# Two graph layers over a 4096 x 4096 adjacency: sums kept in more PSUM banks, more places for tiles, and a fixed order of the second sweep

## Chip, cores and metric

One core of one Trainium2 chip runs the whole program. The metric is the device time of one execution in microseconds (us), lower is better. A profiled execution, taken apart from the timed runs, gives the trace.

## What is computed

N = 4096 nodes, 64 features, a weighted adjacency `adj` (fp32, 67.1 MB) with about 0.8% of its entries not zero.

```python
# layer 0
h = relu(layernorm(x))
for k in range(2):
    agg = adj @ h
    h = tanh(concat([agg, h], 1) @ W[k])
x = x + h
# layer 1
h = relu(layernorm(x))
support = h @ weight
mask = adj != 0
rank = cumsum(mask, axis=1); deg = rank[:, -1:]
k = minimum(deg, 100)
pos = rank - (deg - k)
w = mask * where(pos > 0, 0.5 ** (k - pos), 0)
x = x + w @ support + bias
```

In layer 1 the last nonzero entry of a row weighs 1, the one before it 1/2, and so on.

## The kernel before

**Tiling.** The rows of the result are cut in four chunks of 1024 (index I or g, NCH = 4), the columns in 32 blocks of 128 (b), which also form four chunks of eight (J). A tile is one block against one chunk of rows: 128 x 1024 fp32, 512 KB.

**Sweep 1** (lines 464 to 611) loads all of `adj` once, in pairs of tiles. For each it does hop 1 of layer 0 (and hop 2 where the features of hop 1 are ready already, line 593), and it counts nonzeros, which leaves one byte per entry in `code[g][J]` (8 KB per partition for each of the 16 pairs). Places in these byte arrays that are not yet written serve as tile buffers, as the five pairs of `ring` do.

**Sweep 2** (lines 912 to 1036) does two things side by side.

- *Hops.* 72 tiles are loaded again and multiplied with the features of hop 1: `hop` (line 959) calls `agg_pair` (line 278), two fp32 matmuls of 512 columns. `plan` (line 917) sets their order: row 3 is complete after hop 12, row 2 after hop 24, row 1 after hop 48, row 0 after hop 72. When a row is complete, `finish_x2` (line 660) runs a chain of short steps over TensorE (py, line 678), VectorE, ScalarE and GpSimd that ends with layer 1's features of that chunk, `feats[I]` (lines 724 and 725).
- *Units of layer 1.* 128 units (J, g, n): source chunk J, target rows g, block n of eight. `convert` (line 771) turns 128 x 1024 bytes into fp32r weights, in one ScalarE instruction (Exp, line 791) or in two on VectorE (lines 783 and 786, by way of one scratch tile, `bits`). `layer1` (line 839) then does two matmuls of 128 x 512 (line 851). J runs from 3 down to 0, since row 3's features come first. In some pairs (`kept`, line 761) the sum over J stays in its PSUM banks; after the others `evict` (line 870) copies it to SBUF or adds it there, two VectorE or ScalarE instructions. After J = 0, `finish_out` (line 888) multiplies by the layer's weight (pto, line 899), adds, and stores.

**What sets the order.** The program is scheduled at build time. `clock` holds a planned time for each engine, `use` advances it, and the loop at lines 996 to 1034 picks the next piece of TensorE's work from these clocks: a hop if its tile is planned to have landed, a unit if its weights are planned to be ready, changing from one kind to the other as rules at lines 1004 to 1013 say. 56 units are held back until the hops are over (`n_late`, line 924). `decode` (line 795) places conversions and the last byte subtractions (`settle`, line 452) on ScalarE and VectorE, with limits: how far ahead of TensorE (`lead`, `dlead`), and how near to a waiting chain (`gap`). On the chip each engine runs its own list in that order and waits by semaphores.

**Places.** A converted unit needs a 128 x 1024 fp32r place (`spaces`). They come from ring pairs no longer needed for loads (`consumed`, line 939), from the bytes of pairs (J, g) whose units are done (`pair_space`, line 747, two places each), from `after0`, `after1`, `hx1` and `hx2` when these are read for the last time, and from each unit's own place after its matmuls. `KEEP` = 4 of the five ring pairs go on being loaded. Two pairs' bytes hold `parts`, the sums in SBUF.

**PSUM.** Eight banks: `pacc` two tiles of two banks, `plow` two of one, `pone` the single banks "one" and "two".

**Queues.** All loads of `adj` are issued by SyncE in order: rows 3 to 1 at line 930, row 0, whose DRAM side is rearranged in four short pieces per partition, at line 934; the residual x at line 655; stores at line 909.

Of the kernel before, what the change touches and what calls it, by code (L numbers as in the profile page):

```python
# [19 lines left out]
P = 128  # L20
# [8 lines left out]
LOW = 138  # L29
# [15 lines left out]
def gnn_kernel(  # L45
# [614 lines left out]
    def finish_x2(I, acc):  # L660
# [11 lines left out]
        state["gap"] = 1.35, 2.2  # L672
        yield t

        pt = one(name="py")
# [84 lines left out]
    order = {3: (0, 1, 2, 3), 2: (3, 0, 1, 2), 1: (2, 3, 0, 1), 0: (0, 1, 2, 3)}  # L760
    kept = {(3, 3), (2, 2), (1, 0), (1, 1)}
# [7 lines left out]
    state = {"wide": True, "fetch": True, "done": 0, "lead": 5.0, "dve": False, "dlead": 2.0, "gap": (0.0, 0.0)}  # L769

    def convert(engine=None):
        i = len(made)
        J, g, n = units[i]
        spaces.sort(key=lambda v: v[1])
        w, t = spaces.pop(0)
        v = (J, g, n % 2)
        if v in settled:
            settle(settled.index(v))
            done[J, g] = use("DVE", 1.25)
        t = max(t, done.get((J, g), 0.0) + 0.1)  # L780
        q = code[g][J][:, n, :]
        if engine == "DVE" or not engine and state["dve"] and max(clock["ACT"], t) + 0.96 > max(clock["DVE"], t) + 1.4:
            nc.vector.tensor_scalar(  # L783
                state["bits"], q, float(ZERO), ONE, op0=ALU.subtract, op1=ALU.mult
            )
            nc.vector.tensor_scalar(  # L786
                w, state["bits"].bitcast(F32), 2.0 ** (127 - LOW), None, op0=ALU.mult
            )
            t = use("DVE", 1.4, t)
        else:  # L790
            nc.scalar.activation(w, q, AF.Exp, scale=LN2, bias=BIAS)  # L791
            t = use("ACT", 0.96, t)
        made.append([w, t + 0.1])

    def decode():
        while True:
# [8 lines left out]
            if n < len(units):  # L805
                wanted = {(J, g, k % 2) for J, g, k in units[n : n + 12]}
                soon = [v for v in settled if v in wanted]
            else:
                soon = []
            t = min((v[1] for v in spaces), default=1e9)  # L810
            if n == len(units):
                t = 1e9
            act, dve = (max(clock[e], t) for e in ("ACT", "DVE"))
            late = clock["DVE"] <= clock["PE"] + state["dlead"]
# [4 lines left out]
            elif (  # L819
                state["dve"] and late and dve + 1.4 <= d_end and dve <= clock["PE"] + 3.0  # L820
                and dve + 1.4 < act + 0.96 + (0.0 if len(spaces) < 3 else 1.0)
            ):
                convert("DVE")
            elif act <= min(now, a_end - 0.96):
                convert("ACT")
# [13 lines left out]
    def layer1():  # L839
# [3 lines left out]
        while len(made) <= i:  # L843
            convert()
        J, g, k = units[i]
        if k == 0 and g not in sums:
            sums[g] = pacc.tile([P, NC, C], F32, tag="acc", name="accl")
        first, last = k == 0 and (J + 1, g) not in kept, k == CB - 1 and (J, g) not in kept
        w = made[i][0]
        for c in range(NC):  # L850
            nc.tensor.matmul(  # L851
                sums[g][:, c, :], feats[J][:, k, :], w[:, c * C : (c + 1) * C],
                start=first, stop=last,
            )
# [5 lines left out]
        if 0 < J < NCH - 1 or J and g % 2:  # L860
            pair_space(f"code{g}{J}", t)
        elif J:
            parts[g // 2] = place([P, 2, NC, C], F32, f"code{g}{J}", "parts")
# [6 lines left out]
    def evict(J, g, acc):  # L870
# [3 lines left out]
        for c, p in enumerate(part(g)):  # L874
            if not new:
                nc.vector.tensor_tensor(p, acc[:, c, :], p, op=ALU.add)
                t = use("DVE", 0.7, t)
            elif clock["ACT"] <= clock["DVE"]:
                nc.scalar.copy(p, acc[:, c, :])
                t = use("ACT", 0.65, t)  # L880
            else:
                nc.vector.tensor_copy(p, acc[:, c, :])
# [3 lines left out]
    outs = []  # L886

# [24 lines left out]
    def sweep2(acc):  # L912
        rings = sorted(range(RING // 2), key=lambda k: places[k][2])
        KEEP = 4
# [9 lines left out]
        n_late = 56  # L924
        clock["DMA"] = -10.5

# [12 lines left out]
        def consumed(k, r, a, t):  # L939
            n = len(tiles)  # L940
            if k is None:
                state["bits"] = place([P, CW], U32, "hx0", "bits")
                state["dve"] = True
            elif n < total and (k in rings[-KEEP:] or n < 2 * RING - 2 * (RING // 2 - KEEP)):
                load(k, r, a, t)
            elif k in open_:
                pair_space(f"ring{k}", open_.pop(k), t)
# [3 lines left out]
        for n, k in enumerate(rings):  # L951
            for r in range(2):
                load(k, r, ring[k][:, r, :], 3.5 * (n - RING // 2 + 1))
# [5 lines left out]
        def hop(n):  # L959
            I, b = blocks[n]  # L960
            if I not in accs:
                accs[I] = two(name="acc1") if I == 1 else plow.tile([P, C], F32, tag="low", name="acc1")
# [23 lines left out]
        def runnable(cap, slack):  # L986
            n = 0
            for i in range(state["done"], min(cap, len(made))):
                t = max(ready.get(units[i][0], 1e9), made[i][1])
                if t > clock["PE"] + slack + 0.465 * n:  # L990
                    break
                n += 1
            return n

        n = 0
        while n < total or state["done"] < len(units) or chain or outs:
            run_chain()
            if n < total:
                state["lead"] = min(10.0, 0.86 * (total - n) + 0.2)
                state["dlead"] = min(2.0, state["lead"])  # L1000
            decode()
            if n == total:
                state.update(lead=10.0, dlead=2.0)
            cap = len(units) - (n_late if n < total else 0)
            units_ = runnable(cap, 0.1)
            hops = 0
            while n + hops < min(total, len(tiles)) and tiles[n + hops][3] <= clock["PE"] + 0.1 + 0.86 * hops:
                hops += 1
            if state["wide"]:
                go = 1 if units_ else 2 if hops else 0  # L1010
            else:
# [59 lines left out]
```

## Time and profile before

| | |
|---|---|
| median of 3 runs | 345.52 us (345.49, 345.52, 347.02) |
| the profiled execution's own time | 344.91 us |
| its span, first to last instruction | 343.0 us |
| TensorE matmul busy | 327.8 us (96%) |
| VectorE busy | 280.9 us (82%) |
| ScalarE busy | 197.0 us (57%) |
| HBM read, written | 107.15 MB, 1.05 MB: 315 GB/s over the span |
| last hop ends, last output matmul ends | 301.8 us, 339.5 us |

A page of the profile lists busy time by engine, the span in slices, the DMA queues, the chain of work that ended last, and the costliest groups. In a timeline, a row gives start, duration, engine, line, operation, output and inputs by the program's names, and how many instructions were merged in it; a bracket gives the idle time of the engine before the row and what ended it. One fp32 matmul of a hop shows as two records. Some matmul records are missing from the trace, so counts of them can be a few per cent low.

### The profile page before, as it was taken

What the parts mean: (1) busy time and instruction counts of PE and PEld (TensorE: products, weight loads), DVE (VectorE), ACT (ScalarE), POOL (GpSimd) and SP (SyncE); (2) the same over time, 40 slices, a digit from 0 to 9 for tenths busy, and PEclk for the clock granted to TensorE, in tenths of its full rate; (3) what the DMA queues carried; (4) which work ended last, traced back from release to release, by engine and by line L of the source; (5) the groups of instructions that cost most, each with busy time, mean ns of one, the idle gap of its engine ahead of it and who ended that gap; (6) DMA issues with size and microseconds to landing.
All of it is one profiled execution on the core that took longest, in us unless ns stands there. A gap on an engine that the chain in (4) does not pass through costs nothing.

```text
span 343.0 us, 3882 instructions
## 1 busy us (share of the span) xinstructions
PE 327.8 (96%) x1360; PEld 156.0 (45%) x1360; DVE 280.9 (82%) x440; ACT 197.0 (57%) x206; POOL 24.9 (7%) x23
## 2 busy tenths in 40 slices
PE   2899999999999999999999999999999999998995
PEld 0344334333444444344444343343454656367785
DVE  5799998999869999899998495688266799989953
ACT  2296872654466550474124534137378989979980
POOL 2450000000000000000000000422003000003000
PEclk9999999999999999999999999999999999999998
DMA  7999999999999998966998999999998958600012
GB/s 274 424 419 418 421 421 419 423 418 420 423 421 420 386 389 338 358 234 237 371 327 298 303 369 411 383 410 409 409 373 268 343 134 245 202 0 0 2 50 72
DMA packets 25474, 108.44 MB, mean 316 GB/s; under 512 B 2416, under 2 KB 3824, under 8 KB 17392
## 3 DMA queue, kind: packets, MB, share of 16 engines
q1 hardware_dynamic: 25456, 108.21, 82.7%
q8 instruction: 10, 0.16, 0.2%
q14 instruction: 8, 0.07, 0.0%
HBM read 107.15 MB, written 1.05 MB: 315 GB/s over the span
## 4 chain that ended last, share of the span: by engine, by line
PE 63%; DMA 21%; DVE 8%; ACT 3%; issue 2%; SPq 1%; ACTq 0%; DVEq 0%
PE acc L593 24%; PE acc L280 15%; PE accl L851 12%; DMA codes<-in_adjA_dram 11%; DMA ring<-in_adjA_dram 8%; PE acc_low L280 6%; DMA pre<-in_x_dram 2%; PE pto L899 2%; DVE weights L786 2%; ACT weights L791 2%; PE pt L348 2%; DVE bits L783 2%; PE po L211 1%; DVE mbuf L261 1%; DVE codes L253 1%
## 5 line engine op out<-in xcount | busy, mean ns | idle before, releaser
L791 ACT ACTIVATE weights<-codes 128x1024 fp32r<-128x1024 uint8 x90 | 86.7, 1046 | 12.2 <-PE accl L851 9.6
L593 PE MATMUL acc<-ring,hx 128*128 128x512 f32 x176 | 76.5, 594 | 0.6 <-DMA ring<-in_adjA_dram 0.6
L280 PE MATMUL acc<-ring,hx 128*64 128x512 f32 x288 | 66.8, 599 | 0.8 <-DMA ring<-in_adjA_dram 0.7
L851 PE MATMUL accl<-weights,feat 128*128 128x512 f32 x254 | 63.4, 400 | 1.3 <-DVE feat L725 0.9
L851 PEld LDWEIGHTS accl<-weights,feat 128*128 128x128 f32 x254 | 45.9, 188 | 21.3 <-ACT weights L791 6.6
L593 PEld LDWEIGHTS acc<-ring,hx 128*128 128x128 f32 x176 | 33.2, 190 | 43.8 <-issue 41.5
L456 DVE TENSOR_TENSOR codes<-codes,after 128x2048 uint16<-128x2048 uint16 x32 | 38.3, 1219 | 0.1
L280 PEld LDWEIGHTS acc<-ring,hx 128*64 128x64 f32 x288 | 19.3, 136 | 39.8 <-issue 29.8
L261 DVE TENSOR_SCALAR mbuf<-ring 128x2048 uint8<-128x2048 f32 x30 | 36.6, 1220 | 0.0
L246 ACT ACTIVATE codes<-codes 128x2048 uint8<-128x2048 int8 x18 | 34.4, 1910 | 0.6
L254 DVE TENSOR_SCALAR cnt<-codes 128x1024 uint16<-128x1024 uint16 (+1 forms) x80 | 30.0, 375 | 2.7
L253 DVE TENSOR_TENSOR codes<-mbuf,cnt 128x1024 uint16<-128x1024 uint16 (+1 forms) x51 | 30.6, 599 | 1.8
L786 DVE TENSOR_SCALAR weights<-bits 128x1024 fp32r<-128x1024 f32 x37 | 26.6, 718 | 6.6 <-PE accl L851 3.0
L245 ACT ACTIVATE codes<-ring 128x2048 int8<-128x2048 f32 x8 | 15.3, 1912 | 27.0 <-DMA ring<-in_adjA_dram 27.0
L783 DVE TENSOR_SCALAR bits<-codes 128x1024 uint32<-128x1024 uint8 x37 | 25.6, 691 | 0.8
L245 ACT ACTIVATE codes<-codes 128x2048 int8<-128x2048 f32 x10 | 19.1, 1913 | 11.7 <-DMA codes<-in_adjA_dram 11.6
L699 POOL TENSOR_TENSOR pre<-pre,wb 128x512 f32<-128x512 f32 x4 | 5.5, 1378 | 271.5 <-DVE xc L193 271.5
L280 PE MATMUL acc_low<-codes,hx 128*64 128x512 f32 x104 | 24.9, 594 | 0.1
L280 PE MATMUL acc_low<-ring,hx 128*64 128x512 f32 x88 | 22.3, 598 | 0.0
L545 PE MATMUL acc_low<-ring,hx 128*64 128x512 f32 x40 | 12.3, 745 | 8.3 <-DVE hx L201 6.8
L261 DVE TENSOR_SCALAR mbuf<-codes 128x2048 uint8<-128x2048 f32 x16 | 19.5, 1220 | 0.0
L198 POOL TENSOR_TENSOR s<-s,half 128x8 f32<-128x8 f32 (+1 forms) x10 | 16.9, 1691 | 15.7 <-DVE s L197 15.7
(99 smaller groups left out, 270.0 us busy)
## 6 DMA issues: line engine op xcount, KB each, us to landing
ring<-in_adjA_dram SPq DMA_DIRECT2D x74, 512.0 KB, 8.1
ring<-in_adjA_dram SPq DMA_DIRECT2D x37, 1024.0 KB, 8.0
codes<-in_adjA_dram SPq DMA_DIRECT2D x26, 1024.0 KB, 17.3
pre<-in_x_dram SPq DMA_DIRECT2D x4, 256.0 KB, 6.9
xres<-in_x_dram SPq DMA_DIRECT2D x4, 256.0 KB, 7.9
out_dram<-o SPq DMA_DIRECT2D x3, 256.0 KB, 2.6
out_dram<-o SPq DMA_DIRECT2D x2, 128.0 KB, 2.2
wb<-in_weights_dram SPq DMA_DIRECT2D x1, 192.0 KB, 14.3
```

Source lines behind the costliest of these rows:

```text
L245: nc.scalar.activation(sign, tile_of(I, a), AF.Sign)
L246: nc.scalar.activation(m, sign, AF.Square, scale=float((FLAG - 1 + 0.25) ** 0.5))
L253: nc.vector.tensor_tensor(q, m, cnt, op=ALU.add)
L254: nc.vector.tensor_scalar(cnt, q, 0x7F7F, None, op0=ALU.bitwise_and)
L261: nc.vector.tensor_scalar(m, tile_of(I, a), 0.0, float(FLAG - 1), op0=ALU.not_equal, op1=ALU.mult)
L280: nc.tensor.matmul(acc[c * D : (c + 1) * D, :], src, a[:, c * C : (c + 1) * C], start=first, stop=last,)
L456: nc.vector.tensor_tensor(q, q, a[:, None, :].to_broadcast([P, 4, CW // 2]), op=ALU.subtract)
L593: nc.tensor.matmul(acc[0][:, c, :], at(g), a[:, r, c * C : (c + 1) * C], start=g == CB * I - 1, stop=g == 0,)
L783: nc.vector.tensor_scalar(state["bits"], q, float(ZERO), ONE, op0=ALU.subtract, op1=ALU.mult)
L786: nc.vector.tensor_scalar(w, state["bits"].bitcast(F32), 2.0 ** (127 - LOW), None, op0=ALU.mult)
L791: nc.scalar.activation(w, q, AF.Exp, scale=LN2, bias=BIAS)
L851: nc.tensor.matmul(sums[g][:, c, :], feats[J][:, k, :], w[:, c * C : (c + 1) * C], start=first, stop=last,)
```

## The change

- **PSUM.** Nine of the twelve sums (J, g) with J > 0 are kept in PSUM over J, instead of four; the order of g within J changes. For the pairs (3, 2), (1, 1) and (0, 2) the sum lies in two tiles of `plow` instead of one of `pacc`. Row 0's hop accumulator moves from `plow` to the bank "one", and row 1's py from "one" to "two".
- **Places for tiles.** `more_tiles` turns the bytes of the finished pairs (3, 1), (2, 3), (2, 0) and (1, 0) into two load buffers each; if no load is left, they become places for weights. `KEEP` falls from 4 to 3, so that two ring pairs instead of one become places for weights early.
- **Conversions.** `convert` takes a list of engines. Two conversions on VectorE can be issued as two first halves and then two second halves if there are two scratch tiles in `bits`. A second one would come with the pair `bits_pair`, which is `None` in this version; `hx0` gives one scratch tile.
- **Order.** `steps2` lists (hops done, units done) eight times: hops up to the first number, then units up to the second. The rules on planned landings, `runnable` and `n_late` go.
- `lead` 10 to 6, `dlead` 2 to 3, `gap` ahead of the addition to py 1.35 to 0.5, and VectorE is chosen for a conversion with other margins.

```diff
-        state["gap"] = 1.35, 2.2
+        state["gap"] = 0.5, 2.2
...
-        pt = one(name="py")
+        pt = (two if I == 1 else one)(name="py")
...
-    order = {3: (0, 1, 2, 3), 2: (3, 0, 1, 2), 1: (2, 3, 0, 1), 0: (0, 1, 2, 3)}
-    kept = {(3, 3), (2, 2), (1, 0), (1, 1)}
+    order = {3: (0, 1, 2, 3), 2: (1, 2, 3, 0), 1: (2, 3, 0, 1), 0: (1, 0, 2, 3)}
+    spilled = {(3, 0), (2, 1), (1, 2)}
+    kept = {(J, g) for J in range(1, NCH) for g in range(NCH)} - spilled
+    in_low = {(3, 2), (1, 1), (0, 2)}
...
+        dve = [v for v in made_ if v[0] == "DVE"]
+        n = len(bits)
+        for k, (_, w, t, q) in enumerate(dve):
             nc.vector.tensor_scalar(
-                state["bits"], q, float(ZERO), ONE, op0=ALU.subtract, op1=ALU.mult
+                bits[k - n], q, float(ZERO), ONE, op0=ALU.subtract, op1=ALU.mult
             )
+            use("DVE", 0.65, t)
+        for k, (_, w, t, q) in enumerate(dve):
             nc.vector.tensor_scalar(
-                w, state["bits"].bitcast(F32), 2.0 ** (127 - LOW), None, op0=ALU.mult
+                w, bits[k - n].bitcast(F32), 2.0 ** (127 - LOW), None, op0=ALU.mult
             )
...
             elif (
-                state["dve"] and late and dve + 1.4 <= d_end and dve <= clock["PE"] + 3.0
-                and dve + 1.4 < act + 0.96 + (0.0 if len(spaces) < 3 else 1.0)
+                len(bits) > 1 and late and dve2 + 2.6 <= d_end and dve2 <= clock["PE"] + 3.0 and n + 2 <= len(units)
+                and len(spaces) > 1 and dve2 + 2.6 < act + 1.92 + (0.5 if len(spaces) < 4 else 2.0)
             ):
-                convert("DVE")
+                convert(["DVE", "DVE"])
+            elif (
+                bits and late and dve + 1.5 <= d_end and dve <= clock["PE"] + 3.0
+                and dve + 1.5 < act + 0.96 + (0.5 if len(spaces) < 3 else 2.0)
+            ):
+                convert(["DVE"])
...
-            sums[g] = pacc.tile([P, NC, C], F32, tag="acc", name="accl")
+            if (J, g) in in_low:
+                sums[g] = [plow.tile([P, C], F32, tag="low", name="accl") for _ in range(NC)]
+            else:
+                v = pacc.tile([P, NC, C], F32, tag="acc", name="accl")
+                sums[g] = [v[:, c, :] for c in range(NC)]
...
-        if 0 < J < NCH - 1 or J and g % 2:
+        if (J, g) in ((3, 0), (2, 2)):
+            parts[g // 2] = place([P, 2, NC, C], F32, f"code{g}{J}", "parts")
+        elif (J, g) == bits_pair:
+            v = place([P, 2, CW], U32, f"code{g}{J}", "bits")
+            bits[:] = [v[:, r, :] for r in range(2)]
+            space(place([P, CW], F32R, "hx0", "weights"), clock["DVE"] + 0.1)
+        elif (J, g) in tile_pairs:
+            more_tiles[0](f"code{g}{J}", t)
+        elif J:
             pair_space(f"code{g}{J}", t)
-        elif J:
-            parts[g // 2] = place([P, 2, NC, C], F32, f"code{g}{J}", "parts")
...
+    more_tiles = []
+    bits = []
+    bits_pair = None
+    tile_pairs = {(3, 1), (2, 3), (2, 0), (1, 0)}
...
-        KEEP = 4
+        ring_at = {f"ring{k}": ring[k] for k in rings}
+        rings = list(ring_at)
+        KEEP = 3
+        steps2 = [(25, 4), (32, 10), (35, 12), (39, 30), (49, 39), (55, 40), (58, 56), (72, 128)]
...
+        def more_tiles_(tag, t):
+            v = place([P, 2, CW], F32, tag, "ring")
+            for r in range(2):
+                if len(tiles) < total:
+                    load(tag, r, v[:, r, :], t)
+                else:
+                    consumed(tag, r, v[:, r, :], t)
...
-            elif n < total and (k in rings[-KEEP:] or n < 2 * RING - 2 * (RING // 2 - KEEP)):
+                bits.append(place([P, CW], U32, "hx0", "bits"))
+            elif n < total and (
+                k not in rings[:-KEEP] or n < 2 * RING - 2 * (RING // 2 - KEEP)
+            ):
                 load(k, r, a, t)
...
-                accs[I] = two(name="acc1") if I == 1 else plow.tile([P, C], F32, tag="low", name="acc1")
+                accs[I] = (
+                    plow.tile([P, C], F32, tag="low", name="acc1") if I > 1
+                    else (two if I else one)(name="acc1")
+                )
...
-                state["lead"] = min(10.0, 0.86 * (total - n) + 0.2)
-                state["dlead"] = min(2.0, state["lead"])
+                state["lead"] = min(6.0, 0.86 * (total - n) + 0.2)
+                state["dlead"] = min(3.0, state["lead"])
...
+            while steps2 and n >= steps2[0][0] and state["done"] >= steps2[0][1]:
+                steps2.pop(0)
+            to = steps2[0] if steps2 else (total, len(units))
+            i = state["done"]
-            if len(outs) > 1 or outs and state["done"] == len(units):
+            if len(outs) > 1 or outs and i == len(units):
...
-            elif go == 1:
-                layer1()
-            elif go == 2:
+            elif n < min(to[0], len(tiles)):
                 hop(n)
                 n += 1
+            elif i < to[1] and units[i][0] in ready and (len(made) > i or spaces):
+                layer1()
+            elif chain:
+                clock["PE"] = max(clock["PE"], chain[0][0])
+            elif n < min(total, len(tiles)):
+                hop(n)
+                n += 1
             else:
-                later = [x[0] for x in chain[:1]]
...
+                clock["PE"] += 0.3
```

## The prediction

> **What bounds the kernel now.** I read the page's shares first, then the chain that ended last, TensorE's and ScalarE's timelines for the second sweep, the DMA's part of it and the costliest groups.
>
> The page says TensorE is busy 96% of the span, and the chain of waits is TensorE for 63% of it. Sweep 2 begins at 193.4 us. Two kinds of work alternate on TensorE there: a hop (line 280, two fp32 matmuls, four records) and a layer-1 unit (line 851, two records). From the chain (start, us, what):
>
> ```profile
> 201.44 8.73 PE acc L280 x40
> 234.29 1.87 PE acc L280 x8
> 236.16 1.59 PE accl L851 x6
> 287.46 5.70 PE accl L851 x24
> ```
>
> Ten hops take 8.73 and two 1.87, so a hop costs 0.8575 and each stretch of hops 0.155 to start. Twelve units take 5.70 and three 1.59: 0.457 a unit, 0.22 a start. One hop stretch plus one unit stretch costs 0.375 of starts. TensorE's timeline shows the stalls (in brackets):
>
> ```profile
> 223.53 1.08 PE L280 MATMUL acc<-ring,hx 128*64 128x512 f32 x4 [0.24 <-DMA ring<-in_adjA_dram]
> ...
> 274.52 2.71 PE L851 MATMUL accl<-weights,feat 128*128 128x512 f32 x10 [0.17 <-DVE weights L786]
> ...
> 303.98 1.21 PE L678 MATMUL py<-wz,S 128*128 128x128 f32 x8 [0.49 <-DVE S L669]
> 304.95 10.72 PE L851 MATMUL accl<-weights,feat 128*128 128x512 f32 x46
> 316.60 7.11 PE L851 MATMUL accl<-weights,feat 128*128 128x512 f32 x30 [0.94 <-DVE feat L725]
> 323.87 0.73 PE L851 MATMUL accl<-weights,feat 128*128 128x512 f32 x2 [0.16 <-ACT weights L791]
> ```
>
> They sum to 2.0 us. So TensorE is nearly full, and little can be won without removing its work. Behind it stand the conversions of bytes to weights, ScalarE's timeline:
>
> ```profile
> 242.09 2.95 ACT L791 ACTIVATE weights<-codes 128x1024 fp32r<-128x1024 uint8 x3 [1.81 <-PE accl L851]
> 250.89 1.06 ACT L791 ACTIVATE weights<-codes 128x1024 fp32r<-128x1024 uint8 x1 [5.85 <-PE accl L851]
> ...
> 277.11 27.57 ACT L791 ACTIVATE weights<-codes 128x1024 fp32r<-128x1024 uint8 x29
> ...
> 310.46 22.83 ACT L791 ACTIVATE weights<-codes 128x1024 fp32r<-128x1024 uint8 x24
> ```
>
> Until 251 it waits for places that units give back; later it runs solid. Its rate is 27.57/29 = 0.951 us. On VectorE a conversion is two instructions, and their starts in the chain (270.69, 272.21, 273.77) lie 1.54 apart. Both engines together: 1/0.951 + 1/1.54 = 1.70 per us, 0.59 us each, against TensorE's 0.457. After row 0's last hop the tail runs near this second limit too.
>
> The DMA's part of sweep 2, by stretch (TensorE busy, its clock, DMA share, GB/s come in each row):
>
> ```profile
> 193.40:222.10 28.70, 28.13 (x132) 10.48 (x131) 19.07 (x24) 11.33 (x19) 3.83 (x2) 1.00 1.00 379
> 222.10:301.83 79.73, 79.31 (x347) 39.18 (x345) 59.03 (x86) 60.62 (x67) 7.14 (x4) 1.00 0.87 304
> 301.83:339.46 37.63, 36.02 (x190) 30.11 (x188) 29.03 (x46) 28.75 (x32) 3.25 (x2) 1.00 0.04 14
> ```
>
> Hops up to about 225 wait for the DMA, later ones mostly do not.
>
> **What the Trainium skill says.** "TensorE: Matmul & The Clock Gate", Part 1, gives back-to-back matmuls of 512 columns 215.7 ns; hops agree (8.73/40 = 0.218), units run at 0.2285. "Perfetto Trace Analysis", Identifying the Most-Contended Engine, warns that matmul busy is no measure of headroom; therefore I compare lengths of stretches, not the 96%. "DMA: Bandwidth & Descriptors", Anatomy of one DMA, fits 2.0 us plus bytes/436e3, so 3.2 us for 512 KB; this trace has 4.0 for line 930 with an empty queue (its issues at 179.8), and for row 0 (line 934, issues 278.3 to 280.9) more:
>
> ```profile
> DMA to landing us min/median/max: 5.0/6.8/8.2
> ```
>
> The measurement decides. Row 0's rate is 340 GB/s (window 267 to 276), 1.54 us a tile.
>
> **The change part by part**, from 222.1 us (25 hops done) to the last output matmul at 339.46.
>
> (1) *Work that stays*: 47 hops x 0.8575 = 40.3; 128 units x 0.457 = 58.5; three py groups (line 678) about 1.0 each; output matmuls (line 899) 1.82 + 1.82 + 3.78 = 7.4. Together 109.2. Measured: 117.4. Of the 8.2 over, 12 alternations are 4.5, the named stalls 2.0, and 1.7 remains (starts around py and pto, small waits), which I keep.
>
> (2) *Order*. steps2 has eight alternations: 8 x 0.375 = 3.0 us, **1.5 less**. The 0.94 goes: 72 units now stand behind row 0's last hop, 40 of them free of its features; 40 x 0.457 = 18 us covers the 14.7 us from there to the features (301.83 to 316.5). What is late next is the conversions, see (5). The 0.49, 0.24, 0.17 and 0.16 go with the old order, and new waits take their place.
>
> (3) *Evictions*. Nine of twelve (J, g) sums stay in PSUM instead of four: seven evictions instead of twelve, 14 instructions of 0.68 instead of 24, so 6.8 us less on VectorE and ScalarE. Nothing for TensorE by itself: its bank waits are not in the trace. In the tail it is one eviction fewer (four for five), 1.3 us or 0.8 conversions.
>
> (4) *Tiles*. Ring pairs kept for loads fall from four to three: six tiles in flight instead of eight; the bytes of (3,1) and (2,3) add two each. DMA keeps up through the first steps: six tiles are 6 x 1.28 = 7.7 us of transfer (landings 1.28 apart when saturated), against a cycle of 4.0 + 1.0. After 18 units (8.4 us) it idles, but the tenth hop behind needs only hop 40's reload, 4-5 us old. **The last 14 hops are the place where it costs.** Before them come 16 units (7.5 us), the queue is empty, and (2,3)'s bytes come free only with the last unit. From that moment, tiles 66, 67, ... 71 land at 5.2 and then every 1.5: 5.2, 6.7, 8.2, 9.7, 11.2, 12.7. TensorE reaches them at 7.0, 7.9, 8.7, 9.6, 10.4, 11.3 (0.155 + 0.8575 each). The last hop ends at 13.6 instead of 12.2: **1.4 us** (0.6 at 1.35 a tile, 2.1 at 1.65). SP issues cost 0.37 each and xres comes after them, so they add nothing. Early on, the hop before the 6-unit step waits for a landing much as now: zero difference.
>
> (5) *Conversions*. The pair path needs two bits tiles; bits_pair is None, so only hx0's is ever there: **no pair is made**, and VectorE stays at 1.54 each. Two ring pairs instead of one become weight places early: 4, and 6 with after0 and after1. Units 4 to 9 with four places: the fifth place comes back 0.9 us into the step, conversion 9 on VectorE takes 1.54, wait 0.4. Units 12 to 29: six ready, twelve more at 1.70 per us, 7.1 us from 0.9 in; the step would be 8.4, end 0.5 late. Together **0.9** (0 if the last subtraction of line 456, 235.6, comes earlier; 2 if VectorE is held by chain 2). Tail: at its start places are 24 and about 22 units are ready (8 when the last hops begin, five more at once, then hx2 and ring pairs as hops end). 50 remain for the 38 us until the last unit: ScalarE (38 - 2.5 of tanh, square, copy, gaps)/0.951 = 37; VectorE 38 - 6.2 (chain) - 3.8 (evictions) - 1.4 (outputs) - 2.5 (gaps behind the chain) = 24, /1.54 = 15. 52 for 50: **0.4** of waits (0 to 2.5).
>
> (6) *PSUM and gap*. plow holds (3,2), (1,1), (0,2) in turn; row 2's sum leaves it at 222, (3,2) starts near 243. Row 0's accumulator in "one" moves py of row 1 to "two", already copied: zero, and if it waited, one copy of 0.7. The changed gap and lead only reorder VectorE and ScalarE, -0.3 to +0.7; I take zero.
>
> *Sum*: 109.2 + 3.0 + 1.7 + 1.4 + 0.9 + 0.4 = 116.6 against 117.4, **0.8 us less**: 344.91 - 0.8 = 344.1 on the profiled execution. The runs' median is 0.6 above that execution, where the same gain is 344.7. I forecast **344.4**.
>
> **The rivals.** *A, full packing*: places come early enough and no new wait appears; 109.2 + 3.0 + 1.7 = 113.9, 3.5 less, 341.4 to 342.0; half of it is 343. For it: ScalarE idles before 251, so earlier places help, and every new stall above is under 1.5. Against: the 5.0 us landing and two engines short of TensorE's pace by 0.13 us a unit.
> *B, slower: the tail starves of weights.* The list leaves 72 units to the end (58 now) and does not go back to hops when weights are missing. Each conversion short costs 0.59. If 14 instead of 22 are ready at the last hop, because ring pairs come free late, eight less two of slack cost 3.6: about 348. From 6 to 7 conversions short it decides. For it: ScalarE already solid from 310 to 333. Against: 5.3 to 6.8 us of eviction time saved.
> *C, it does not do what it says*: for the pairs that is so, and is in the sum.
>
> **How the numbers follow.** Unchanged as summed 0.42 (its own range 343.2 to 346.4), A 0.40, B 0.18. A change below 0.5%, 1.7 us, cannot be told from none here. Range 341.3 to 347.3: it takes in A's full sum nearly and B's first half. Chances faster 0.40, same 0.42, slower 0.18.
>
> **What would show it.** Right: eight alternations; 14 evictions; no two line-783 successors in a row; row 0's last hops waiting on ring DMA for 1 to 2 us; features of row 0 no longer a wait; line 851 waiting on weights for under 2 us. Wrong: no DMA wait in the last hops (A), or TensorE waiting more than 3 us on weights after them (B).

## The result, and the profile after

The changed kernel takes 349.34 us (median of 4 runs, 349.0 to 349.91), the kernel before 345.51 (4 runs, 345.49 to 347.02): a ratio of 1.0104, 95% interval 1.0077 to 1.0132. It is slower by about 3.8 us, where 0.8 less was forecast, and it lies 2 us above the range.

In the profiled executions the times are 349.91 and 344.91. TensorE's timeline cuts that difference in three:

| us | before | after |
|---|---|---|
| sweep 2's first hop starts at | 193.41 | 194.12 |
| from there to py of row 2 (line 678, after 25 hops) | 28.66 | 32.78 |
| from there to the start of the last output matmuls (line 931, before 899) | 113.45 | 113.40 |

The first row is sweep 1, which the change leaves alone; among all 14 profiled executions below it lies between 192.98 and 194.84, so a difference of a microsecond there, or in the time of one profiled execution, says nothing. **The loss is in the second row: 4.1 us before any unit of layer 1 has run.** The third row, in which everything that the prediction put a cost on happens, is as long as before.

Busy time by stage in the changed kernel, cut at those two places and at the first unit after the last hop (columns: length of the stage; PE, PEld, DVE, ACT, POOL busy with their counts; TensorE's granted clock as a share of full speed; the DMA share; GB/s):

```profile
194.12:226.90 32.78, 30.05 (x131) 10.67 (x130) 19.06 (x24) 13.22 (x21) 3.83 (x2) 0.93 0.95 353
226.90:302.71 75.81, 73.38 (x319) 35.05 (x317) 47.72 (x70) 51.64 (x56) 7.07 (x4) 0.99 0.91 313
302.71:344.29 41.58, 41.58 (x218) 35.63 (x216) 31.60 (x49) 37.03 (x41) 3.25 (x2) 1.00 0.04 13
```

Against the three rows of before (in the prediction), the first stage has a DMA that is not full (0.95 for 1.00) and a TensorE clock of 0.93 for 1.00. The tail's TensorE is without a gap: 41.58 busy of 41.58. Its timeline, in lines that matter below:

```profile
211.96 7.37 PE L280 MATMUL acc<-ring,hx 128*64 128x512 f32 x32
221.34 1.30 PE L280 MATMUL acc<-ring,hx 128*64 128x512 f32 x4 [2.01 <-DMA ring<-in_adjA_dram]
223.29 3.68 PE L280 MATMUL acc<-ring,hx 128*64 128x512 f32 x8 [0.66 <-DMA ring<-in_adjA_dram]
226.90 2.08 PE L678 MATMUL py<-wz,S 128*128 128x128 f32 x8
...
265.50 1.08 PE L280 MATMUL acc<-ring,hx 128*64 128x512 f32 x4 [0.54 <-DMA ring<-in_adjA_dram]
...
276.23 1.08 PE L280 MATMUL acc<-ring,hx 128*64 128x512 f32 x4 [0.81 <-DMA ring<-in_adjA_dram]
...
304.60 24.79 PE L873 MATMUL accl<-weights,feat 128*128 128x512 f32 x108
```

Two things are to be seen. First, hops wait for a landing at 219.3 and 222.6, and then two hops take 3.68 us where a row of two takes 1.94 elsewhere, and py 2.08 for 1.21. Second, after row 0's last hop 54 units (108 records) run as one row: neither features nor weights hold TensorE up.

Why did no tile land? SyncE's loads of `adj` issued between 207.5 and 213.9 (count, ns, first and last start), in the changed kernel:

```profile
L972 SPq DMA_DIRECT2D ring<-in_adjA_dram x1: 328/328/328, 207.5 to 207.5; - x1
```

The same window in the kernel before:

```profile
L930 SPq DMA_DIRECT2D ring<-in_adjA_dram x3: 327/328/328, 210.2 to 213.2; - x3
```

After the load at 207.5 comes none until 213.9. The code says why. In the first turn tiles 0 to 9 lie in the five ring pairs and tile 10 in `hx0`; tile 11 goes where hop 0 has been, and so on. `hx0` is not loaded again, and `consumed` gives a ring pair up when its second turn comes: with `KEEP` = 4 that is pair 0 alone, hops 11 and 12; with 3 it is pairs 0 and 1, hops 11 to 14. So hops 10 to 14 (counted from 0), five in a row, free no buffer for a load, where it was three. What follows, in slices of 6 us (TensorE busy, clock, DMA share, GB/s), in the changed kernel:

```profile
214.00:220.00 6.00, 5.27 (x24) 1.00 0.77 227
220.00:226.00 6.00, 4.00 (x12) 0.67 1.02 414
226.00:232.00 6.00, 6.00 (x26) 0.76 0.85 336
```

Two of these slices in the kernel before:

```profile
214.00:220.00 6.00, 5.74 (x28) 1.00 1.02 389
220.00:226.00 6.00, 5.44 (x26) 1.00 1.01 386
```

In the slice behind the gap the DMA moves 227 GB/s instead of 389, TensorE then waits, and its clock falls to half for the hops behind the wait. The two parts can be told apart. The tile of hop 24, the last one ahead of py, lands at 224.53, 30.4 us into sweep 2; before, it lands at 220.93, 27.5 us into it. That is 2.9 of the 4.1 us. From this landing to py it is 2.37 us instead of 1.14, at half clock: the other 1.2.

### The profile page after: what moved, and what is told of

Its sections match the earlier page's. It is cut to its first block, busy times and chain, and to the rows that moved or that the text cites. A ratio compares the mean times of both kernels' runs of the same rounds, so it can differ in the third digit from the quotient of the medians.

```text
span 347.8 us, 3874 instructions
## 1 busy us (share of the span) xinstructions
PE 328.3 (94%) x1360; PEld 157.2 (45%) x1360; DVE 273.3 (79%) x428; ACT 198.2 (57%) x207; POOL 24.7 (7%) x23
## 4 chain that ended last, share of the span: by engine, by line
PE 81%; DMA 15%; SPq 2%; ACT 1%; issue 1%; DVE 0%; DVEq 0%
PE acc L593 24%; PE accl L873 17%; DMA ring<-in_adjA_dram 15%; PE acc_low L280 12%; PE acc L280 10%; PE acc L545 4%; PE po L211 2%; PE pto L931 2%; PE acc_low L545 2%; PE acc L385 2%; PE pt L348 2%; PE py L678 1%; SPq L137 1%; PE ph L302 1%; PE pt L374 1%; ACT weights L788 1%
## 5 line engine op out<-in xcount | busy, mean ns | idle before, releaser
L788 ACT ACTIVATE weights<-codes 128x1024 fp32r<-128x1024 uint8 x91 | 87.9, 1044 | 12.0 <-PE accl L873 5.5
L280 PE MATMUL acc<-ring,hx 128*64 128x512 f32 x288 | 69.3, 614 | 5.1 <-DMA ring<-in_adjA_dram 5.1
L873 PE MATMUL accl<-weights,feat 128*128 128x512 f32 x254 | 61.5, 396 | 0.0
L873 PEld LDWEIGHTS accl<-weights,feat 128*128 128x128 f32 x254 | 46.6, 188 | 15.8 <-ACT weights L788 3.9
L798 DVE TENSOR_SCALAR weights<-bits 128x1024 fp32r<-128x1024 f32 x36 | 25.0, 695 | 12.2 <-PE acc L280 5.2
L793 DVE TENSOR_SCALAR bits<-codes 128x1024 uint32<-128x1024 uint8 x36 | 24.9, 693 | 1.0
L280 PE MATMUL acc_low<-ring,hx 128*64 128x512 f32 x88 | 22.3, 598 | 0.0
L545 PE MATMUL acc_low<-ring,hx 128*64 128x512 f32 x40 | 11.3, 690 | 10.8 <-DVE hx L201 7.1
```

The source lines that it names most:

```text
L280: nc.tensor.matmul(acc[c * D : (c + 1) * D, :], src, a[:, c * C : (c + 1) * C], start=first, stop=last,)
L545: nc.tensor.matmul(low0[c][h * D : (h + 1) * D, :], at(b)[:, :D], part_of(a, b), start=b >= NB - 2 if c == 0 else k == 8 and b > 1, stop=b ...
L798: nc.vector.tensor_scalar(w, bits[k - n].bitcast(F32), 2.0 ** (127 - LOW), None, op0=ALU.mult)
L873: nc.tensor.matmul(sums[g][c], feats[J][:, k, :], w[:, c * C : (c + 1) * C], start=first, stop=last,)
```

## The experiments

Theories. *Loads*: the places taken from loads let the DMA run dry at turns of the buffers, early and in later steps. *Weights* (rival B): the fixed list or the missing places leave TensorE without converted units. *Clock*: the waits are small, the half clock behind them is the loss. *Places*: loads and weights share the same bytes, and what one gains the other loses.

In the table, A is sweep 2's first hop to py of row 2, B from there to the start of the last output matmuls, both of one profiled execution each. "Hops over" and "units over" are how much longer the hop and unit stretches of sweep 2 are than 0.155 + 0.8575 a hop and 0.22 + 0.457 a unit, worked out row by row from the timeline; waits and a low clock are in it, and a wait ahead of a stretch's first row counts to the stretch before it. Ratios are timed against the kernel before, with 95% intervals. A profiled execution can lie well off its median (a_pairs: 352.09 us, median 348.86; a_keep4: 354.2 and 352.37; a_late: 349.84 and 348.1), so a difference of two or three microseconds in one B says little.

| | ratio | A | B | hops over | units over |
|---|---|---|---|---|---|
| before | 1 | 28.66 | 113.45 | 1.7 | 2.4 |
| after | 1.0104 (1.0077 to 1.0132) | 32.78 | 113.40 | 9.9 | -0.3 |
| a_keep4 | 1.0222 (1.0195 to 1.0248) | 28.71 | 121.63 | 6.5 | 8.0 |
| a_late | 1.0083 (1.0052 to 1.0114) | 30.07 | 116.05 | 7.7 | 2.4 |
| a_fill | 1.0127 (1.0098 to 1.0157) | 31.82 | 113.16 | 6.3 | -0.4 |
| b_psum | 1.0121 (1.0085 to 1.0157) | 28.35 | 116.45 | 5.6 | 0.0 |
| a_spread | 1.0036 (1.0016 to 1.0056) | 28.41 | 114.88 | 7.3 | 0.3 |
| a_oldlist | 1.0152 (1.0118 to 1.0187) | 29.24 | 118.50 | 5.0 | 5.0 |
| a_pairs | 1.0115 (1.0074 to 1.0157) | 32.72 | 116.17 | 13.6 | -0.4 |
| a_evict | 1.0161 (1.0123 to 1.0199) | 31.37 | 117.16 | 11.3 | 1.4 |
| a_oldlist_nt | 1.0012 (0.9990 to 1.0033) | 29.51 | 113.47 | 3.3 | 2.0 |
| a_tiles | 1.0014 (0.9994 to 1.0035) | 28.28 | 112.85 | 4.3 | 1.0 |
| a_even | 1.0011 (0.9995 to 1.0028) | 28.50 | 113.94 | 5.5 | 0.4 |
| a_both | 0.9923 (0.9897 to 0.9949) | 28.62 | 110.88 | 3.1 | 0.1 |

A falls into two groups. In the four kernels in which two ring pairs leave the loads at hops 11 to 14 (after, a_fill, a_pairs, a_evict) it is 31.4 to 32.8; in the others it is 28.3 to 29.5, with a_late at 30.07.

### Four ring pairs for loads again

```diff
-        KEEP = 3
+        KEEP = 4
```

> The changed kernel with KEEP = 4 again: one ring pair, not two, leaves the loads at hops 11 and 12; TensorE's order is the same. Loads theory (the two pairs taken at hops 11 to 14 let the DMA run dry, TensorE waits 2.7 us and then runs at half clock for some 6 us): the gap goes, 4 us less than the changed kernel, 345 us, clock 1.00 from 222 to 229. List theory (the fixed order and weights too late in the long tail cost the time): no change here, 349, or above it, since two places for weights are missing. Clock theory (the clock falls by itself): 349 with the clock still at 0.5.

Measured: 352.37 us. The early loss is gone (A 28.71, as before), and the kernel is slower still. The timeline, from py of row 2:

```profile
224.85 1.09 PE L873 MATMUL accl<-weights,feat 128*128 128x512 f32 x4
229.82 0.73 PE L873 MATMUL accl<-weights,feat 128*128 128x512 f32 x2 [3.88 <-ACT weights L788]
230.49 7.92 PE L280 MATMUL acc<-ring,hx 128*64 128x512 f32 x28
```

The fourth unit has no weights for 3.88 us, since the list asks for four units before hop 26 and the second pair of places is not there; then seven hops take 7.92 where they should take 6.16 (0.155 + 7 x 0.8575), with a granted clock of 0.81 from 232 to 238 us. That ties the early loss to the pair given up, and shows what it was given up for: the list needs those places. Loads and places hold; weights holds for this version alone.

### The pairs given up one turn later

```diff
-                k not in rings[:-KEEP] or n < 2 * RING - 2 * (RING // 2 - KEEP)
+                k not in rings[:-KEEP] or n < 26
```

> The changed kernel with the bound on the early loads at 26 instead of 16: all five ring pairs are loaded again at hops 11 to 14, and two of them become places for weights ten hops later, at hops 21 to 24. TensorE's order is the same. Loads theory: as with four pairs kept, 345 us or a little less (344 to 345.5), since later there are as many places for weights as in the changed kernel. List theory: 349 or more, as the first places come ten hops later.

Measured: 348.1 us. Of the 4.1 us in A, 2.7 come back (30.07), and B is 2.65 longer: the places come later to the weights, and TensorE waits 1.9 us on them. So it seems to move the conflict and not to end it, as far as one execution, 1.7 us above the median, can say. Its interval overlaps that of the changed kernel, so no gain over that is shown.

### TensorE kept busy through the wait

Three useless matmuls into the free bank "one" are added, two of 512 columns ahead of hop 22 and one of 256 ahead of hop 23; the result is unaffected.

```diff
+        idle_ = []
...
+            if n == 22:
+                idle = one(name="idle")
+                idle_.append(idle)
+                for _ in range(2):
+                    nc.tensor.matmul(idle, ident, flat(hxs[3])[:, :C], start=True, stop=True)
+            if n == 23:
+                nc.tensor.matmul(idle_[0][:, :256], ident, flat(hxs[3])[:, :256], start=True, stop=True)
```

> The changed kernel with three matmuls more, of no use, into the free bank one: two ahead of hop 22 and a half one ahead of hop 23, where TensorE waits for loads. The loads stay as they are. Loads theory with the clock as its second half: TensorE is busy in the wait, the clock stays at 1.00, hops 23 and 24, py and the first units take their usual time, 2 to 2.4 us less, 347 us. If the lower clock costs nothing beside the wait: 349.3, or later by the added work (up to 2 us).

Its timeline at the same place:

```profile
219.05 1.98 PE L1016 MATMUL idle<-hx,ident 128*128 128x512 f32 x4
221.12 1.08 PE L280 MATMUL acc<-ring,hx 128*64 128x512 f32 x4
222.12 0.70 PE L1018 MATMUL idle<-hx,ident 128*128 128x256 f32 x2
...
225.34 1.21 PE L678 MATMUL py<-wz,S 128*128 128x128 f32 x8
```

The wait is filled, hops and py behind it run at full speed, and the mean clock of this execution is 1.00 (0.986 in that of the changed kernel). A becomes 31.82 instead of 32.78. Hop 22 begins 27.6 us into sweep 2 instead of 27.2, so the filling itself may hold it up by 0.4.

That the filling kept the clock up is not shown by this one execution. `a_evict` (below) has the same hops and loads up to here and no filling, waits as follows, and its granted clock is 1.00 from 220 to 228 us all the same:

```profile
220.31 1.08 PE L280 MATMUL acc<-ring,hx 128*64 128x512 f32 x4 [1.46 <-DMA ring<-in_adjA_dram]
222.25 1.08 PE L280 MATMUL acc<-ring,hx 128*64 128x512 f32 x4 [0.87 <-DMA ring<-in_adjA_dram]
```

Its A is 31.37. For the filling speaks that all six timed executions of this version have a mean clock of 0.996 or more, and the four of the changed kernel 0.993 or less. In both cases of full clock 2.7 to 3.2 us of the 4.1 stay, since the tiles are not there earlier, and 1.0 to 1.4 go with the clock, which agrees with the 2.9 and 1.2 above. Timed, 348.83 us can't be told from 349.34. Clock falls as the main cause; the low clock follows the wait.

### Only the PSUM part, in the kernel before

The lists `order`, `kept` and `in_low`, the accumulators and py's bank of the changed kernel; its seven evictions with them. The planner of before stays, and packs the work in another order, in 18 stretches of units where it had 16. (The expectation's "10 fewer evictions" are five fewer, ten instructions.)

```diff
-    order = {3: (0, 1, 2, 3), 2: (3, 0, 1, 2), 1: (2, 3, 0, 1), 0: (0, 1, 2, 3)}
-    kept = {(3, 3), (2, 2), (1, 0), (1, 1)}
+    order = {3: (0, 1, 2, 3), 2: (1, 2, 3, 0), 1: (2, 3, 0, 1), 0: (1, 0, 2, 3)}
+    spilled = {(3, 0), (2, 1), (1, 2)}
+    kept = {(J, g) for J in range(1, NCH) for g in range(NCH)} - spilled
+    in_low = {(3, 2), (1, 1), (0, 2)}
...
```

> The kernel before with the PSUM part alone: nine sums kept, order of g, three sums in plow, row 0's accumulator and row 1's py moved; the planner chooses the order of hops and units as before. Prediction's view: nothing on TensorE's path, 10 fewer evictions leave VectorE and ScalarE 6.8 us, 345.5 within 1 us, at best 1.5 less. If the banks make new waits: above 347.

Measured: 349.15 us. No unit waits for a bank (units over 0.0). What grew is the hops, 5.6 over, 4.6 of it waits on the DMA, among row 0's last hops:

```profile
300.29 1.08 PE L280 MATMUL acc<-ring,hx 128*64 128x512 f32 x4 [1.35 <-DMA ring<-in_adjA_dram]
304.25 1.08 PE L280 MATMUL acc<-ring,hx 128*64 128x512 f32 x4 [1.54 <-DMA ring<-in_adjA_dram]
```

The run changes two things at once, sums and the planner's order, so it doesn't price the sums; the run with before's order (below) does.

### Two pairs that do not leave one behind the other

```diff
-                k not in rings[:-KEEP] or n < 2 * RING - 2 * (RING // 2 - KEEP)
+                k not in (rings[0], rings[3]) or n < 2 * RING
```

Still two ring pairs are given up, in their second turn, but pairs 0 and 3: hops 11, 12 and 17, 18 free no buffer, hops 13 to 16 do.

> The changed kernel with the same number of ring pairs for loads and for weights, but the two pairs leave the loads apart from each other: the first at hops 11 and 12, the other at hops 17 and 18, so that hops 13 to 16 go on issuing loads. TensorE's order is the same. Loads theory (four hops in a row without an issue let the DMA run dry): the DMA stays busy from 214 to 220, TensorE comes to its first units some 29 us after the start of sweep 2 instead of 32.8, and no half clock there: 345.5 us, 3 to 4 less than the changed kernel. Places theory (any ring pair less for loads costs the same, or the first units then wait for weights): 348 to 350.

Measured: 346.25 us (22 runs), 3.1 us below the changed kernel (2.3 by the two ratios, whose intervals don't meet), and A is 28.41, that of before. In the slices of 6 us the DMA no longer runs dry and the clock stays:

```profile
214.00:220.00 6.00, 5.82 (x28) 1.00 1.04 396
220.00:226.00 6.00, 5.73 (x30) 1.00 0.99 366
```

The number of buffers is the same, only the moments at which they leave differ. This is the closest test of the early loss, and loads holds. What is left above before, 1.0036, is in B: hops wait 3.5 us for the DMA.

### The old list on the new places, and without the new load places

`a_oldlist` takes four ring pairs and the alternations that the kernel before had; `a_oldlist_nt` takes also the four pairs of bytes away from the loads, so that TensorE and SyncE have the order of before, with the new sums and margins of conversion.

```diff
-        KEEP = 3
-        steps2 = [(25, 4), (32, 10), (35, 12), (39, 30), (49, 39), (55, 40), (58, 56), (72, 128)]
+        KEEP = 4
+        steps2 = [(26, 3), (30, 5), (33, 6), (35, 9), (39, 14), (46, 19), (48, 27), (54, 34), (56, 48), (60, 58), (62, 70), (72, 128)]
```
```diff
-    tile_pairs = {(3, 1), (2, 3), (2, 0), (1, 0)}
+    tile_pairs = set()
```

> The changed kernel with KEEP = 4 and, as steps2, the twelve changes that the planner of the kernel before had made (26 hops then 3 units, 30 and 5, 33 and 6, 35 and 9, 39 and 14, 46 and 19, 48 and 27, 54 and 34, 56 and 48, 60 and 58, 62 and 70, 72 and 128). Loads and places theory (the order asked for units before there were places for their weights, and KEEP = 4 alone did not help for that reason): 345 us, at best 344. If the PSUM part or the other margins cost by themselves: 348 or more.

> The changed kernel with KEEP = 4, the twelve changes of the kernel before as steps2, and no finished bytes as load buffers (tile_pairs empty: they all become places for weights). TensorE's order and the loads are then those of the kernel before; what is left of the change is the PSUM part and the margins for VectorE. Places theory (the 5 us of waits for weights in the run with the old order came from the bytes of (3,1) that went to loads): 345 us, at best 344, waits for weights back to about 2 us. If PSUM or margins cost by themselves: 348 or more.

Measured: 350.7 and 345.52 us. TensorE's waits in sweep 2 of the first (us in total, times, longest):

```profile
PE accl L873 <- DVE weights L798: 2.0, 2, 1.8
PE accl L873 <- ACT weights L788: 1.9, 3, 1.0
PE acc L280 <- DMA ring<-in_adjA_dram: 0.9, 4, 0.3
```

In the second the weights hold it up by 1.1 us. The two differ in nothing but the bytes of four finished pairs: given to loads under the old order they cost 5 us. Of that, 2.8 are waits on weights (3.9 for 1.1), whose places they were; behind the wait of 1.8 us the granted clock is 0.57 from 266 to 270 us. The second run is the price of the PSUM part, of the new margins, `gap` and `lead` together: none that can be measured. So under this order the fewer evictions, 7 for 12, bring nothing that shows; a gain that the margins took back isn't ruled out.

### Pairs of conversions, and more evictions

```diff
-    bits_pair = None
+    bits_pair = (2, 1)
```
```diff
-    kept = {(J, g) for J in range(1, NCH) for g in range(NCH)} - spilled
+    kept = {(3, 1), (3, 2), (3, 3)}
```

> The changed kernel with bits_pair = (2, 1), so that VectorE's conversions come in pairs from the middle of sweep 2 on, and one place for weights fewer. TensorE's order is the same. If weights are not what TensorE waits for in the changed kernel, as its trace says: no change, 349 within 0.7. If VectorE's rate binds the tail: 1 us less or better.

> The changed kernel with only the three sums of J = 3 kept in PSUM: 13 evictions instead of 7, 12 instructions of 0.68 us more on VectorE and ScalarE, 8.2 us; orders of TensorE and of the loads are the same. The prediction's step on evictions (nothing on TensorE's path by itself, 0.59 us for each conversion that the tail then lacks beyond two): 349 to 351, and TensorE's waits on weights grow by that. If evictions never reach TensorE: 349.3 within 0.7.

With a second scratch tile: 348.86 us, the same as the changed kernel. In the trace first and second halves still alternate there, so that no true pair was tried; the starts of two conversions lie 1.43 us apart (285.32, 286.75) instead of 1.54. Weights were not what TensorE waited for; in this execution, 3.2 us above the median, it waits 7.4 us on the DMA.

With 13 evictions for 7: 350.95 us, above the changed kernel's 349.34, though the intervals of the two ratios touch. Six more evictions are 12 instructions of about 0.68, 8.2 us of VectorE and ScalarE; on TensorE 0.65 us of waits on weights appears, and 6.8 us of waits on the DMA against 5.1. So the sums in PSUM may be worth some two microseconds in this version, which these runs don't establish.

### A further load place, and another list

Each starts from the version with pairs 0 and 3. `a_tiles` adds (3, 3) to the pairs whose bytes are lent to loads; `a_even` spreads the units over ten steps; `a_both` takes the further place and a list of nine steps.

```diff
-    tile_pairs = {(3, 1), (2, 3), (2, 0), (1, 0)}
+    tile_pairs = {(3, 1), (3, 3), (2, 3), (2, 0), (1, 0)}
```
```diff
-        steps2 = [(25, 4), (32, 10), (35, 12), (39, 30), (49, 39), (55, 40), (58, 56), (72, 128)]
+        steps2 = [(25, 4), (32, 10), (35, 12), (39, 20), (44, 30), (49, 36), (54, 44), (58, 52), (63, 60), (72, 128)]
```
```diff
-        steps2 = [(25, 4), (32, 10), (35, 12), (39, 30), (49, 39), (55, 40), (58, 56), (72, 128)]
+        steps2 = [(25, 4), (29, 8), (33, 12), (39, 26), (45, 34), (51, 42), (57, 52), (63, 60), (72, 128)]
```

The first diff belongs to `a_tiles` and `a_both`, the second to `a_even`, the third to `a_both`.

> The run with ring pairs leaving apart, and the bytes of (3,3) as two load buffers more instead of two places for weights, from the middle of the 18-unit stretch on. TensorE's order is the same. Loads theory for the later part (hops behind 18 and 16 units find too few tiles loaded, 6.3 us over their length there): 2 to 4 us of it go, 343 to 345 us, if the weights stay in time. Places theory: as much comes back as waits for weights, 346 to 348.

> The run with ring pairs leaving apart, and ten changes in smaller steps instead of eight: (39, 20), (44, 30), (49, 36), (54, 44), (58, 52), (63, 60) stand for (39, 30), (49, 39), (55, 40), (58, 56). No stretch of units is longer than ten before row 0's last hops, so the load buffers never stay full for long. Loads theory: two alternations cost 0.75, 3 us of hop waits go, 343.5 to 345 us. If the order matters little: 346 to 347.

> The run with ring pairs leaving apart and the bytes of (3,3) as load buffers, with eight changes in more even steps: (25, 4), (29, 8), (33, 12), (39, 26), (45, 34), (51, 42), (57, 52), (63, 60), then (72, 128). Loads theory: of the hop waits of those two runs (4.3 and 5.5 us over sweep 2) some 2 are left, waits for weights under 1, two more half alternations cost 0.4: 343.5 to 344.5 us, under both kernels. If a wait only moves from loads to weights: 345.5 within 0.7.

Measured: 345.4, 345.75 and 343.13 us. The further place alone and the ten-step list alone end at the time of before, not under it as expected. The further place with the nine-step list makes a kernel 0.8% (0.5 to 1.0) faster than the one before. The nine-step list was not run without the further place, so how much of this is the list and how much needs both stays open. The largest stretch of the changed kernel without hops, 18 units at 248 us, empties the load queue. Two slices behind it, in the changed kernel:

```profile
252.00:258.00 6.00, 5.98 (x27) 1.00 0.83 332
258.00:264.00 6.00, 6.00 (x32) 1.00 0.71 159
```

The same two in `a_both`:

```profile
252.00:258.00 6.00, 6.00 (x28) 1.00 0.96 330
258.00:264.00 6.00, 6.00 (x30) 1.00 0.98 335
```

The DMA's share is 0.71 where it is 0.98 in the other. SyncE is through with its loads of tiles at 286.5 us in `a_both`, 91.7 after its sweep 2 began, and at 294.6 in the changed kernel, 100.5 after. The hops' waits on the DMA fall from 5.1 us to 1.0, and the units stay without waits (0.2).

## Why the prediction was wrong

The account of the profiles closes: against before, hops over +8.2, units over -2.6, starts of stretches -1.5, together +4.1; A and B differ by 4.12 - 0.05 = 4.1. Of the hops' 8.2, half lies in A; the other half, in B, eats up what the units and the starts win there.

- **The step that failed is (4), tiles: "DMA keeps up through the first steps ... zero difference".** It reckoned six tiles in flight in a steady cycle, and began at 222.1 us. The loss comes from the turn in which the pairs leave, ten microseconds earlier: five hops in a row free no buffer, no load is issued from 207.50 to 213.94, and the next loads land at 218.20, 221.29 and 223.25. Hops wait 2.0 and 0.7 us, hop 24's tile comes 2.9 us later than before, and half clock adds 1.2 ahead of py (and some 0.9 in py itself, 2.08 for 1.21, which is in B). Shown by the version in which pairs 0 and 3 leave: A goes back from 32.78 to 28.41.
- **(4), later hops: mis-sized.** From py of row 2 on the hops are over by 4.1 us (before: 0.1); 1.4 was forecast, all of it in the last 14 hops. Those run nearly free (13 hops in 11.38 us, then 0.18 of wait). The waits lie at 247, 265.5, 276, 277 and 281. The one at 265.5 is the tenth hop behind the 18 units, whose reload I had found "4-5 us old" and so in time: it was issued at 258.99 and landed 6.4 us later. In the last 14 hops two things were better than forecast. The bytes of (2,3) were no brake: their loads go out at 285.5, while the last unit of these pairs ends at 290.1, since bytes come free when the conversions have read them, not "with the last unit". And row 0's tiles land 1.35 us apart while the queue is full (276.19 to 291.07, 12 tiles), not 1.5; the window from which I took 1.54 lies behind a gap in the issues.
- **(1), (2) right.** Eight stretches of units; the named stalls are gone, row 0's features among them, and 8 x 0.375 of starts are left, 1.5 us less than with twelve, as stated.
- **(3) right.** Seven evictions, fourteen instructions near the forecast 0.68 us, and TensorE has no wait on a bank. The groups of the three eviction lines (out<-in xcount | busy us, mean ns | idle before, releaser):

```profile
L910 DVE COPY parts<-accl 128x512 f32<-128x512 f32 x6 | 4.0, 686 | 5.1 <-PE accl L873 5.1
L904 DVE TENSOR_TENSOR parts<-accl,parts 128x512 f32<-128x512 f32 x6 | 3.8, 683 | 0.0
L907 ACT COPY parts<-accl 128x512 f32<-128x512 f32 x2 | 1.2, 586 | 1.8 <-DVE parts L910 1.8
```

- **(5) right on the pairs, too dear on the waits.** No pair is made. TensorE waits on weights for about 0, against 0.9 + 0.4. Step (6), zero, holds: the old order with the new sums times at 1.0012 (0.9990 to 1.0033).
- **The sum** from 222.1 on, 116.6 for 117.4, came out at 117.4 (226.90 to 344.29). That it missed by 0.8 only is luck in part: (4) was 2.7 too small, (5) 1.3 too large, and some 0.6 more fell out of the small terms. It was the stage ahead of it, left out of the sum, that decided.
- **Rival B fell.** The forecast of "slower" rested on a tail without weights. There is none: 54 units in one row. The rival's 348 us is near the measured time for another reason, so it is no support.

Of the Trainium skill's statements, the fit in "DMA: Bandwidth & Descriptors", Anatomy of one DMA, is given there for DMAs that GpSimd issues, a condition that the prediction left out. As an estimate from it, 512 KB take 3.2 us; SyncE's loads here took 3.8 and 4.1 us (issued at 258.13 and 231.89), and the next ones more; the measurement decides. Neither these nor the prediction's 4.0 at 179.8 had an empty queue: an earlier load was still to land. "TensorE: Matmul & The Clock Gate", Part 1, says that TensorE idle for a window of about 3.4 us is set to half clock, and is back after as long a time busy. The trace has the half clock (0.50 to 0.52 from 222 to 228 us), but behind waits of 2.0 and 0.66 us with a hop between them. The way back agrees better, as the last section shows.

What stays open: why the landings behind a gap in the issues are so far apart (below), why some waits bring the clock down and others don't, and how much of the difference between 5.0 us of the two profiled executions and 3.8 of the medians is clock. Of the changed kernel's four executions the three others show a mean clock of 0.993, the profiled one 0.986; their own timelines are not known.

## What to carry to other kernels

Where buffers are taken from loads, write down the order in which they leave, hop by hop: a steady count of tiles in flight says nothing on the turn in which two leave in succession. Here such a gap of 6.4 us in the issues cost 2.7 to 4.1 us (A of four kernels against 28.66), in a stage that waits for the DMA. Start the sum at the first instruction whose order changes, not at the first new piece of work. Buffers for loads and places for weights are one store here: four pairs of bytes given to loads cost 5 us under the old list. So an order of work and the places are best chosen together (345.4 and 345.75 us for one place or one list more, 343.13 for a place and another list).

## What the runs showed of the hardware

- **Behind a gap in the issues, landings are far apart.** Behind a gap of 4.9 us the changed kernel issues loads at 231.89, 232.75 and 233.61 us, with one earlier load still to land (at 232.85); they land at 236.01, 239.23 and 240.51. Behind one of 9.0 us it issues at 258.13, 258.99 and 259.85, again with one to land (at 259.05); they land at 261.9, 265.36 and 268.88, the last two being row 0's tiles in short pieces. So once or twice 3.2 to 3.5 us pass between two landings, where 1.28 is usual with a full queue. Behind the gap of 6.4 us that ended at 213.94 it is 3.1 once (218.20 to 221.29). I had taken the second landing for one rate behind the first, 1.28 or 1.5. It isn't always so: in the kernel before, loads issued at 294.21 and 295.07 land at 299.25 and 300.69.
- **TensorE's clock can fall behind short waits, and not behind all.** 2.01 and 0.66 us of waits on tiles were followed by a granted clock of 0.50 from 222 to 228 us; a_pairs has 0.79 from 298 to 306 us behind a wait of 2.18, and a_oldlist 0.57 from 266 to 270 behind one of 1.82. In a_keep4 waits of 0.21 and 1.16 with a unit between them were enough (0.57 from 275 to 279). But a_evict keeps 1.00 behind waits of 1.46 and 0.87, and from 274 to 282 behind one of 1.75. So the length of the wait alone doesn't decide it.
- **Half clock lasted 3.4 us, or twice that.** Worked out from the granted clock in slices of 1 us: 3.4 us in each of the two falls of a_keep4, the two of a_pairs and the one of a_oldlist, and 6.8 in the changed kernel.
